# A two-layer graph network on one core: merges of gathered sums in two float32r parts, one more range of early products, and another planned landing time

## The chip, the cores and the metric

The kernel runs on one core of one Trainium2 chip. The metric is device time in microseconds for one execution. All timed runs compute the whole network, from the inputs in DRAM to the normalized output in DRAM.

## The reference

A graph isomorphism network (GIN) of two layers with a residual connection and a layer norm. There are N = 6250 nodes with D = 256 features, E = 100,000 edges sorted by destination, and a hidden width H = 512. Destinations are dense at low node numbers (node = 6250 u^2 for uniform u), sources are uniform.

```
def gin_agg(h, src, dst, eps):
    agg = segment_sum(h[src], dst, num_segments=N)
    return (1.0 + eps) * h + agg

h = gin_agg(x, src, dst, eps1)          # N x 256
h = relu(h @ W1a + b1a)                 # N x 512
h = relu(h @ W1b + b1b)                 # N x 512
h = gin_agg(h, src, dst, eps2)          # N x 512
h = relu(h @ W2a + b2a)                 # N x 512
y = x + (h @ W2b + b2b)                 # N x 256
out = (y - mean(y)) / sqrt(var(y) + 1e-5)
```

All values are float32.

## The kernel before, in words

**Tiles.** Nodes are cut into 49 tiles of 128 rows. The eight lowest tiles ("heavy") receive about 40% of the edges. For them no row is gathered: layer 1 counts, for every source node and every heavy destination node, how many edges go from one to the other (`counting`, one-hot matmuls), and the sums of heavy tiles are then products of this count matrix with the rows. The products of layer 1 (`first_products`, L1823) run in two passes of four heavy tiles each; each pass waits for its counts. The edges of all other tiles, 474 chunks of 128, are gathered by indirect DMA that GpSimd issues (L525), 128 rows at a time; in layer 1 five of the chunks are loaded row by row by the sync engine instead, so 469 are gathered there and 474 in layer 2.

**Sums of gathered rows.** Chunks form groups. For each group a one-hot matrix `sel` and a placement matrix `to` are made on VectorE. TensorE sums gathered rows into 32-row slots of a PSUM bank (L1206), and `merge` moves this partial sum to node rows: ScalarE copies it from PSUM to `split`, TensorE multiplies it with `to` (L1269), and VectorE adds the result to the accumulators of the tiles that the group reaches (L1279). In layer 1 a merge takes two groups at a time, 2 x 256 columns, with a float32 copy and one float32 matmul a group; the profile records each float32 matmul as two. In layer 2 a merge takes one group of 512 columns, and the copy rounds to float32r; VectorE subtracts it from the bank (L1260) and gives the second, lower part, and two float32r matmuls add up both parts.

**Dense work.** When all contributions of a block of one or two tiles are in, `dense` transposes it (L1323), multiplies with the first weight (L1392) and the second (L1425), and finishes: in layer 1 bias and relu on VectorE and ScalarE and a store of h1 to DRAM from ScalarE's queue (L1442); in layer 2 residual, layer norm and the store of the output from the sync queue.

**Products of layer 2** (`second_products`). The 49 source tiles are 13 ranges of four (the last has one tile). For each range its rows of h1 are loaded (`xr`, sync queue, L1510; two buffers), split into two float32r parts `upper` and `xr` by ScalarE and VectorE (L1587, L1588, L1592), the counts are loaded (`ci`, sync queue, L1613) and cast by ScalarE to `cf` (L1631), and for each of the eight heavy tiles one group of up to eight matmuls of 512 columns is run (L1704) and added to `whole_acc` (L1649; the first time a copy, L1644). The first `AHEAD2` ranges in the order 12, 11, 10, ... are done within layer 1, at priority 6, the lowest; the rest in layer 2 at priority 3. Within layer 1, from shortly before the last gathered rows are planned to have landed (`quiet`), no further product, cast or split of these is placed until the last dense block of layer 1 is placed (`settled`). The buffers `xr` and `upper` turn round over both layers: a range takes the buffer of the range two before it.

**Order.** Nothing of this order is chosen at run time. Each engine runs its instructions as they were written, and a planner (`Plan`) writes them: it plays all processes against a model of costs. A process asks for an engine with a cost and a priority (`("on", "PE", cost, priority)`, lower goes first), for a buffer (`"get"`), or for an event (`"until"`). Gathers are modelled by a pace (`GATHERS`) and a time from the end of the last issue of a piece to its landing (`LANDINGS`, for layer 1 and layer 2). A piece is up to four gathers; six pieces have a place, and the gather that reuses a place waits for the sum that read it. In layer 2 up to three pieces are summed in one turn. SP issues its loads in the order in which the planner came to them, and a load that waits holds back those behind it.

**Between the layers.** The first 24 gathers of layer 2 (`fore`) read h1 without tiles 7 and 8, which are the last ones that layer 1 stores; the contribution of these two tiles is added by matmuls (`adding_late`). So these gathers can start when all other tiles are stored. A zero row of h1 stands in for rows of tiles 7 and 8.

The planner's constants that the change touches:

```
AHEAD2 = 3                # ranges of layer 2's products done in layer 1
LANDINGS = (5.0, 6.0)     # planned landing after the issue, layer 1, layer 2
```

Of the kernel before, what the change touches and what calls it, by code (L numbers as in the profile page):

```python
# [17 lines left out]
P = 128  # L18
# [24 lines left out]
SPLITS = 2  # L43
TILES = 2
# [11 lines left out]
AHEAD2 = 3  # L56
# [15 lines left out]
def dve(n):  # L72
    return 0.085 + 0.00105 * n
# [126 lines left out]
LANDINGS = (5.0, 6.0)  # L200
# [14 lines left out]
BEGINS = (0.0, -40.0)  # L215
FREES = ({"PE": 20.0, "DVE": 22.0, "ACT": 24.0}, {"PE": -4.0, "DVE": -4.0, "ACT": -4.0})
# [159 lines left out]
def tile_gin_residual_layernorm(  # L376
# [176 lines left out]
    def opening(prep, bank, at):  # L553
# [31 lines left out]
        empty = prep.tile([1, H], F32, name="empty")  # L585
        nc.vector.memset(empty, 0.0)
        nc.scalar.dma_start(h1[GAP : GAP + 1, :], empty)
# [22 lines left out]
        def zeroing(of, i):  # L610
            k = slice(i * size, min((i + 1) * size, NT))
            to = of[:, k, :].bitcast(F32)
            nc.scalar.activation(
                to, zero_[:, 0:1].unsqueeze(2).to_broadcast(list(to.shape)), AF.Copy
            )

        for i in range(ZEROS):
            zeroing(at[0], i)
        for i in range(EARLY):
            zeroing(at[1], i)  # L620
# [78 lines left out]
        sloti = prep.tile([P, NCP - NC2], I, name="sloti")  # L699
        nc.vector.tensor_scalar(sloti, dsti, SLOTS - 1, None, op0=ALU.bitwise_and)  # L700
        nc.vector.tensor_copy(slot, sloti)
# [8 lines left out]
        within = prep.tile([P, NG], I, name="within")  # L710
        nc.vector.tensor_scalar(within, headi, SLOTS - 1, None, op0=ALU.bitwise_and)
        turn = prep.tile([P, NG], I, name="turn")
        nc.vector.scalar_tensor_tensor(turn, within, part32, above, op0=ALU.is_gt, op1=ALU.add)
        turned = prep.tile([P, NG], I, name="turned")
        nc.vector.tensor_scalar(turned, turn, PARTS - 1, None, op0=ALU.bitwise_and)
        nc.vector.tensor_scalar(home, turned, float(SLOTS), part32, op0=ALU.mult, op1=ALU.add)
# [5 lines left out]
        wb = prep.tile([P, NG], I, name="wb")  # L722
        nc.vector.tensor_scalar(wb, basei, P - 1, None, op0=ALU.bitwise_and)
        own = prep.tile([P, NG], F32, name="own")
        nc.vector.scalar_tensor_tensor(own, wb, part, tb, op0=ALU.is_gt, op1=ALU.add)
# [101 lines left out]
    def ordered(ctx):  # L827
# [45 lines left out]
        def layer(number, pools, table, width, scale, weights, ba, wide, at=None, aside=None, right=None):  # L873
# [50 lines left out]
            def fetch_rows(i):  # L924
# [13 lines left out]
            to_room = Tiles(keep, [P, 2, P], F32 if once else F32R, "to", 5)  # L938
            split_room = Tiles(
                keep if once else hold, [P, 2, width], F32 if once else F32R, "split",  # L940
# [300 lines left out]
            def merge(gs, shared):  # L1241
                ap = bank[shared.number]
                n = len(gs)
                token = yield ("get", split_room, 0)
                split = token.tile
                yield ("on", "ACT", act(n * width), 0)
                if once:
                    if gs[0][2] == gs[-1][2]:
                        used = gs[0][2]
                        nc.scalar.copy(  # L1250
                            split[:used, :n, :].rearrange("p a b -> p (a b)"), ap[:used, : n * width]
                        )
                    else:
                        for i, (g, to, used, _) in enumerate(gs):
                            nc.scalar.copy(split[:used, i, :], ap[:used, i * width : (i + 1) * width])
                else:
                    used = gs[0][2]
                    nc.scalar.copy(split[:used, 0, :], ap[:used])  # L1258
                    yield ("on", "DVE", dve(width), 0)
                    nc.vector.tensor_tensor(  # L1260
                        split[:used, 1, :], ap[:used], split[:used, 0, :], op=ALU.subtract
                    )
                shared.release()
                united = yield ("get", banks, 0)
                yield ("on", "PE", MERGE[number - 1] + n * width * (4 if once else 2) * PASS, 1)
                pu = bank[united.number]
                for i, (g, to, used, to_token) in enumerate(gs):
                    for l in (i,) if once else range(2):
                        nc.tensor.matmul(  # L1269
                            pu[:, i * width : (i + 1) * width], to[:used], split[:used, l, :],  # L1270
                            start=(once or l == 0), stop=(once or l == 1),
                        )
                    to_token.used()
                token.release()
                for i, (g, to, used, _) in enumerate(gs):
                    for t in reach(g):
                        yield ("until", ready[t])
                        yield ("on", "DVE", dve(width), 1)
                        nc.vector.scalar_tensor_tensor(  # L1279
                            acc[t], pu[:, i * width : (i + 1) * width], mask[:, t - lo[g], g : g + 1],  # L1280
                            acc[t], op0=ALU.mult, op1=ALU.add,
                        )
                        settle(t)
                united.release()
# [1265 lines left out]
```

## Time and profile before

| | us |
|---|---|
| median of 3 runs | 1271.05 |
| lowest, highest | 1269.08, 1276.44 |
| the profiled execution | 1268.54 |
| its span, first to last instruction | 1266.8 |

| engine | busy us | share of the span | instructions |
|---|---|---|---|
| TensorE matmul (PE) | 1179.4 | 93% | 6204 |
| TensorE weight load (PEld) | 777.3 | 61% | 6204 |
| VectorE (DVE) | 819.1 | 65% | 2096 |
| ScalarE (ACT) | 654.2 | 52% | 1367 |
| GpSimd (POOL) | 906.8 | 72% | 956 |

The profile is of one execution. Times in its rows are microseconds from the start of the span, durations of single instructions are nanoseconds where a row says "mean ns". Matmuls are pipelined: the time that one costs in a row of them is the distance from start to start, not its duration. Layer 1 fills the span up to about 626, layer 2 the rest. PEclk is the granted TensorE clock as a share of full speed. `q` behind an engine's name means its queue, which issues DMAs and waits.

### The profile page before, as it was taken

The page shows a single profiled execution, that of the slowest core. Times are in us where ns is not written, and L with a number is a line of the kernel's source. Part 1 is how long each engine was busy: PE and PEld are TensorE (multiplying, and loading weights), DVE is VectorE, ACT ScalarE, POOL GpSimd, SP SyncE. Part 2 cuts the span into 40 slices and gives each one's busy share as a digit, 9 for nine tenths or more (in the row PEclk, how much of TensorE's full clock was granted, in tenths as well). Part 3 has the DMA queues.
Part 4 walks back from the last instruction along what each step waited for, and adds up shares of the span by engine and source line. Part 5 has one row for each costly group of instructions (what it writes and reads, how often), then busy time and mean ns, then how long its engine had stood idle before and what let it go on. Part 6 is the DMA issues. An engine that isn't in the chain of part 4 may idle for free. (4 is left out here: it accounts for less than half of the span.)

```text
span 1266.8 us, 21197 instructions
## 1 busy us (share of the span) xinstructions
PE 1179.4 (93%) x6204; PEld 777.3 (61%) x6204; DVE 819.1 (65%) x2096; ACT 654.2 (52%) x1367; POOL 906.8 (72%) x956
## 2 busy tenths in 40 slices
PE   5879899999999999999789899999979999999997
PEld 4345455665555665566446675767756766777676
DVE  7989998878769643333257668769846556645424
ACT  7756679987885764444354334334324434432122
POOL 6777777777777777776477777777777777777730
PEclk9989999999999999999979999999999999999999
DMA  6445466775457776654598888889888888877741
GB/s 213 142 139 151 127 196 202 213 210 159 148 156 210 212 222 202 224 185 128 165 318 301 287 281 273 249 287 308 272 301 259 285 289 254 284 226 243 211 134 48
DMA packets 137646, 276.06 MB, mean 218 GB/s; under 512 B 21754, under 2 KB 68673, under 8 KB 137526
## 3 DMA queue, kind: packets, MB, share of 16 engines
q0 software_dynamic: 60432, 185.79, 48.0%
q1 hardware_dynamic: 43012, 56.43, 13.3%
q10 hardware_dynamic: 34082, 32.43, 7.9%
q8 instruction: 52, 0.85, 0.3%
q14 instruction: 68, 0.56, 0.1%
HBM read 248.95 MB, written 25.62 MB: 217 GB/s over the span
## 5 line engine op out<-in xcount | busy, mean ns | idle before, releaser
L525 POOL DMA_INDIRECT early<-in_x_dram,srcs x469 | 450.0, 960 | 146.4 <-issue 122.8
L525 POOL DMA_INDIRECT early<-h,places x226 | 216.8, 959 | 68.9 <-issue 57.9
L525 POOL DMA_INDIRECT late<-h,places x224 | 214.4, 957 | 68.2 <-issue 56.7
L1279 DVE SCALAR_TENSOR_TENSOR acc<-bank,mask,acc 128x256 f32<-128x256 f32 (+1 forms) x352 | 201.4, 604 | 58.1 <-PE bank L1269 56.1
L1425 PE MATMUL bank<-w1b_s,ht 128*128 128x512 f32 (+1 forms) x392 | 183.6, 597 | 2.9 <-ACT ht L1402 1.9
L1704 PE MATMUL bank<-upper,cf 128*128 128x512 f32 (+1 forms) x392 | 172.3, 440 | 0.9 <-DVE xr L1592 0.9
L1704 PE MATMUL bank<-xr,cf 128*128 128x512 f32 (+1 forms) x392 | 158.2, 404 | 0.6 <-DVE xr L1592 0.5
L1392 PE MATMUL bank<-zt,w2a_s 128*128 128x256 f32 (+2 forms) x736 | 151.2, 359 | 1.2 <-ACT zt L1351 1.2
L1206 PE MATMUL bank<-early,sel 128*32 128x256 f32 (+1 forms) x1414 | 125.8, 470 | 26.5 <-DMA early<-h,places 9.9
L1392 PEld LDWEIGHTS bank<-zt,w2a_s 128*128 128x128 f32 x736 | 127.7, 191 | 27.1 <-ACT split L1258 5.0
L1631 ACT CAST cf<-ci 128x512 fp32r<-128x512 uint8 (+1 forms) x104 | 61.4, 594 | 156.4 <-PE bank L1704 126.6
L1649 DVE TENSOR_TENSOR whole_acc<-bank,whole_acc 128x512 f32<-128x512 f32 x96 | 65.1, 683 | 77.2 <-PE bank L1704 77.1
L1823 PE MATMUL bank<-cf,xh 128*128 128x512 f32 x392 | 110.5, 420 | 4.6 <-DVE xh L1762 4.5
L1425 PEld LDWEIGHTS bank<-w1b_s,ht 128*128 128x128 f32 (+1 forms) x392 | 71.1, 189 | 67.6 <-issue 57.5
L1894 ACT ACTIVATE ca<-numbers,low 128x128 f16<-128x128 f16 x308 | 98.1, 391 | 26.7 <-PE bank L1946 22.5
L1269 PE MATMUL bank<-split,to 128*128 128x512 f32 (+2 forms) x332 | 99.3, 416 | 9.6 <-ACT split L1250 6.2
L1060 DVE TENSOR_TENSOR sel<-iota,slot 128x256 f32<-128x256 f32 (+2 forms) x112 | 49.1, 439 | 90.6 <-PE bank L1206 86.4
L1402 ACT ACTIVATE ht<-bank,b2a_s 128x256 f32<-128x256 f32 (+2 forms) x92 | 36.9, 446 | 134.4 <-PE bank L1392 134.4
L1206 PEld LDWEIGHTS bank<-early,sel 128*32 128x32 f32 x1414 | 38.4, 111 | 101.3 <-issue 57.9
L1392 PE MATMUL bank<-zt,w1a_s 128*128 128x256 f32 (+2 forms) x432 | 96.6, 369 | 3.8 <-ACT zt L1351 2.5
L1915 DVE TENSOR_SCALAR cb<-numbers,si 128x490 f16<-128x490 f16 (+8 forms) x308 | 89.0, 332 | 7.6 <-PE bank L1946 7.3
L1704 PEld LDWEIGHTS bank<-upper,cf 128*128 128x128 f32 (+1 forms) x392 | 75.8, 193 | 25.4 <-issue 4.3
(205 smaller groups left out, 1822.1 us busy)
## 6 DMA issues: line engine op xcount, KB each, us to landing
raw<-in_x_dram ACTq DMA_DIRECT2D x48, 256.0 KB
h<-h1r ACTq DMA_DIRECT2D x48, 256.0 KB
b2b_c<-in_x_dram SPq DMA_DIRECT2D x640, 1.0 KB
xr<-h SPq DMA_DIRECT2D x10, 1024.0 KB
acc<-h SPq DMA_DIRECT2D x17, 512.0 KB
early<-in_x_dram,srcs POOLq DMA_INDIRECT x469
ci<-counts SPq DMA_DIRECT2D x24, 256.0 KB
acc<-in_x_dram SPq DMA_DIRECT2D x21, 256.0 KB
```

The source lines that it names most:

```text
L525: nc.gpsimd.indirect_dma_start(out=rows_[:, j, :], out_offset=None, in_=table, in_offset=bass.IndirectOffsetOnAxis(ap=rows_in[:, c - first ...
L1206: mm = nc.tensor.matmul(pm[b * SLOTS : (b + 1) * SLOTS], sel[:, c - groups[g][0], :], rows_[:, l, :], start=(c == part[0]), stop=(c == par ...
L1269: nc.tensor.matmul(pu[:, i * width : (i + 1) * width], to[:used], split[:used, l, :], start=(once or l == 0), stop=(once or l == 1),)
L1279: nc.vector.scalar_tensor_tensor(acc[t], pu[:, i * width : (i + 1) * width], mask[:, t - lo[g], g : g + 1], acc[t], op0=ALU.mult, op1=ALU.add,
L1392: nc.tensor.matmul(ph[:, (f - o) * TILES * P : (f - o) * TILES * P + nb], wa[:, k, f * P : (f + 1) * P], zt[:, k, :nb], start=(k == 0), st ...
L1425: nc.tensor.matmul(po[:m], ht[:, f, i * P : i * P + m], wb[:, f, :], start=(f == 0), stop=(f == KH - 1),)
L1631: nc.scalar.copy(cf_token.tile[:, : n * P].rearrange("p (k j) -> p k j", j=P), token.tile[:, :n, a : a + P],)
L1649: nc.vector.tensor_tensor(sums_of[t], bank[token.number][:, :width], sums_of[t], op=ALU.add)
L1704: nc.tensor.matmul(bank[token.number][:, :width], cf[:m, j * P : (j + 1) * P], of[:m, j, :], start=(j == 0 and of is upper), stop=(j == le ...
L1823: nc.tensor.matmul(bank[tokens[f].number][:, :c], xh[:m, j, l, f * P : (f + 1) * P], cf[:m, :c], start=(k == 0 and l == 0), stop=(k == NT ...
L1894: nc.scalar.activation(token.tile[:, j, :], numbers[:, :P], AF.Abs, bias=low[:, q * BATCH + j : q * BATCH + j + 1],)
L1915: made = nc.vector.tensor_scalar(token.tile[:, : NT * width_of[c]], numbers[:, : NT * width_of[c]], spot[:, c : c + 1], None, op0=ALU.is_e ...
```

## The change

It does five things.

1. In layer 1, merges that the planner places after 160 us (`PARTED`) use the scheme of layer 2: ScalarE's copy rounds to float32r, VectorE subtracts it from the bank for a second part, and two float32r matmuls a group replace the one in float32. A merge of two groups makes one copy and one subtraction over 512 columns where both groups use the same number of rows. Earlier merges stay in float32. `split` gets room for both parts of both groups (`SIZE`), `to` is float32r in both layers, and layer 1 has four `to` buffers where it had five.
2. `AHEAD2` is 4: range 9 of layer 2's products is placed in layer 1 too, after ranges 12, 11 and 10.
3. `LANDINGS` for layer 2 is 9.0: the planner takes gathered rows to land 3 us later than before.
4. The zero row of h1 is stored from a cleared part of the counts tile instead of a tile of its own; the store moves on ScalarE's queue from ahead of the `dst` loads to behind the clearing of the counts.
5. Five integer tiles of the opening are overwritten in place.

```diff
-AHEAD2 = 3
+AHEAD2 = 4
-LANDINGS = (5.0, 6.0)
+LANDINGS = (5.0, 9.0)
+SIZE = (2, 1)
+PARTED = 160.0
...
-        empty = prep.tile([1, H], F32, name="empty")
-        nc.vector.memset(empty, 0.0)
-        nc.scalar.dma_start(h1[GAP : GAP + 1, :], empty)
...
         for i in range(ZEROS):
             zeroing(at[0], i)
+        empty = at[0][0:1, : size - size % 4, : H].bitcast(F32)
+        n = min(H // empty.shape[2], empty.shape[1])
+        assert n * empty.shape[2] == H
+        nc.scalar.dma_start(
+            h1[GAP : GAP + 1, :].rearrange("a (k n) -> a k n", n=empty.shape[2]), empty[:, :n, :]
+        )
...
-            to_room = Tiles(keep, [P, 2, P], F32 if once else F32R, "to", 5)
+            to_room = Tiles(keep, [P, 2, P], F32R, "to", 4 if once else 5)
             split_room = Tiles(
-                keep if once else hold, [P, 2, width], F32 if once else F32R, "split",
+                keep if once else hold, [P, 2, SIZE[number - 1] * width], F32R, "split",
                 SPLITS if once else 3,
             )
...
-                if once:
-                    if gs[0][2] == gs[-1][2]:
...
+                if gs[0][2] == gs[-1][2]:
+                    parts = [(gs[0][2], slice(0, n * width))]
+                else:
+                    parts = [
+                        (used, slice(i * width, (i + 1) * width))
+                        for i, (g, to, used, _) in enumerate(gs)
+                    ]
+                parted = not once or plan.now > PARTED
+                for used, at_ in parts:
+                    to_ = split[:used, 0, at_]
+                    nc.scalar.copy(to_ if parted else to_.bitcast(F32), ap[:used, at_])
+                if parted:
+                    yield ("on", "DVE", dve(n * width), 0)
+                    for used, at_ in parts:
+                        nc.vector.tensor_tensor(
+                            split[:used, 1, at_], ap[:used, at_], split[:used, 0, at_],
+                            op=ALU.subtract,
+                        )
                 shared.release()
                 united = yield ("get", banks, 0)
-                yield ("on", "PE", MERGE[number - 1] + n * width * (4 if once else 2) * PASS, 1)
+                yield (
+                    "on", "PE", MERGE[number - 1] + n * width * (2 if parted else 4) * PASS, 1
+                )
...
-                    for l in (i,) if once else range(2):
+                    at_ = slice(i * width, (i + 1) * width)
+                    for l in range(2) if parted else (0,):
+                        lhs, rhs = to[:used], split[:used, l, at_]
+                        if not parted:
+                            lhs, rhs = lhs.bitcast(F32), rhs.bitcast(F32)
                         nc.tensor.matmul(
-                            pu[:, i * width : (i + 1) * width], to[:used], split[:used, l, :],
-                            start=(once or l == 0), stop=(once or l == 1),
+                            pu[:, at_], lhs, rhs, start=(l == 0), stop=(l == 1 or not parted),
                         )
```

## Rows read from the trace of the kernel before

**Rows 1.** The page's chain that ended last, shares of the span by engine.

```profile
PE 35%; DVE 6%; DMA 4%; POOL 2%; issue 1%; ACT 1%; DVEq 0%; ACTq 0%; POOLq 0%
```

**Rows 2.** Timeline of POOL: start, us, instruction, idle before and what ended it.

```profile
616.91 0.94 POOL L525 DMA_INDIRECT early<-h,fore  x1 [17.71 <-PE bank L1392]
...
1214.88 0.95 POOL L525 DMA_INDIRECT late<-h,places  x1 [0.30 <-issue]
```

**Rows 3.** Windows: stretch, length, each engine's busy us, PEclk, DMA share, GB/s.

```profile
160.00:400.00 240.00, 230.56 (x1240) 140.89 (x1241) 194.06 (x550) 201.57 (x462) 181.97 (x191) 1.00 0.62 184
500.00:607.00 107.00, 104.20 (x519) 65.86 (x518) 35.96 (x65) 45.52 (x96) 75.13 (x80) 0.98 0.56 177
626.00:640.00 14.00, 4.92 (x25) 0.62 (x24) 3.12 (x8) 2.59 (x5) 10.65 (x12) 0.65 0.99 351
640.00:700.00 60.00, 58.87 (x300) 36.54 (x297) 43.88 (x96) 32.46 (x61) 45.68 (x48) 0.94 0.90 305
945.00:1110.00 165.00, 163.59 (x870) 116.87 (x869) 99.69 (x202) 66.85 (x126) 124.80 (x133) 1.00 0.85 273
1216.00:1267.00 51.00, 42.85 (x302) 38.46 (x294) 15.76 (x47) 13.00 (x39) 0.00 (x0) 0.98 0.12 39
```

**Rows 4.** Timeline of PE between the layers.

```profile
617.22 7.03 PE L1425 MATMUL bank<-w1b_s,ht 128*128 128x512 f32 x16
...
623.68 0.79 PE L1704 MATMUL bank<-upper,cf 128*128 128x512 f32 x1
...
625.71 0.40 PE L1704 MATMUL bank<-xr,cf 128*128 128x512 f32 x1
627.40 1.07 PE L1206 MATMUL bank<-early,sel 128*32 128x512 f32 x8 [1.29 <-issue]
633.87 1.94 PE L1206 MATMUL bank<-early,sel 128*32 128x512 f32 x8 [5.41 <-DMA early<-h,fore]
...
640.06 0.80 PE L1704 MATMUL bank<-upper,cf 128*128 128x512 f32 x1
```

**Rows 5.** Timeline of the sync queue there; idle between merged issues is inside.

```profile
609.51 17.00 SPq L1510 DMA_DIRECT2D xr<-h  x2
626.62 15.39 SPq L1613 DMA_DIRECT2D ci<-counts  x3
```

**Rows 6.** Timeline of ACT there.

```profile
637.41 0.62 ACT L1631 CAST cf<-ci 128x512 fp32r<-128x512 uint8 x1 [11.77 <-DMA ci<-counts]
```

**Rows 7.** Windows of line 1269 alone: PE and PEld busy (records).

```profile
160.00:400.00 240.00, 18.89 (x72) 13.04 (x72) 1.00 0.62 184
400.00:612.00 212.00, 9.93 (x38) 7.11 (x38) 0.99 0.62 189
```

**Rows 8.** Chain of waits in order of time: start, us, what.

```profile
674.94 7.48 PE bank L1704 x32
...
783.42 3.45 PE bank L1392 x16
...
1254.85 1.78 PE bank L1392 x16
```

**Rows 9.** Groups of layer 2 by line and shape: busy, mean ns, idle before.

```profile
L1260 DVE TENSOR_TENSOR split<-bank,split 128x512 fp32r<-128x512 f32 x82 | 53.4, 682 | 16.2 <-ACT split L1258 16.2
...
L1631 ACT CAST cf<-ci 128x512 fp32r<-128x512 uint8 x80 | 49.4, 619 | 124.8 <-PE bank L1704 107.2 <-DMA ci<-counts 11.8 <-issue 5.0
```

**Rows 10.** Line 1704 alone: ns min/median/max, first and last start us.

```profile
L1704 PE MATMUL bank<-upper,cf x392: 389/396/988, 532.6 to 1201.1; 128*128 128x512 f32 x192, 106*128 106x512 f32 x4
```

**Rows 11.** What PE waited for in layer 2: us, times, longest.

```profile
PE bank L1206 <- DMA early<-h,places: 9.9, 4, 4.8
...
PE bank L1206 <- DMA late<-h,places: 1.8, 1, 1.8
```

**Rows 12.** Timeline of PE near the end.

```profile
1223.21 0.71 PE L1269 MATMUL bank<-split,to 128*128 128x512 f32 x2
...
1241.21 0.60 PE L1323 MATMUL bank<-ident,apart 128*128 128x128 f32 x4
```

More of the change, by code (lines that the diff above doesn't have):

```diff
@@ L698, in opening @@
         nc.vector.tensor_copy(dsti, dp[:, : NCP - NC2])
-        sloti = prep.tile([P, NCP - NC2], I, name="sloti")
-        nc.vector.tensor_scalar(sloti, dsti, SLOTS - 1, None, op0=ALU.bitwise_and)
-        nc.vector.tensor_copy(slot, sloti)
+        nc.vector.tensor_scalar(dsti, dsti, SLOTS - 1, None, op0=ALU.bitwise_and)
+        nc.vector.tensor_copy(slot, dsti)
         nc.vector.tensor_tensor(
@@ L709, in opening @@
         nc.vector.tensor_scalar(above, headi, 5, None, op0=ALU.arith_shift_right)
-        within = prep.tile([P, NG], I, name="within")
-        nc.vector.tensor_scalar(within, headi, SLOTS - 1, None, op0=ALU.bitwise_and)
+        nc.vector.tensor_scalar(headi, headi, SLOTS - 1, None, op0=ALU.bitwise_and)
         turn = prep.tile([P, NG], I, name="turn")
[L713 to L716, printed above, removed]
+        nc.vector.scalar_tensor_tensor(turn, headi, part32, above, op0=ALU.is_gt, op1=ALU.add)
+        nc.vector.tensor_scalar(turn, turn, PARTS - 1, None, op0=ALU.bitwise_and)
+        nc.vector.tensor_scalar(home, turn, float(SLOTS), part32, op0=ALU.mult, op1=ALU.add)
         basei = prep.tile([P, NG], I, name="basei")
@@ L721, in opening @@
         nc.vector.tensor_scalar(tb, basei, 7, None, op0=ALU.arith_shift_right)
-        wb = prep.tile([P, NG], I, name="wb")
-        nc.vector.tensor_scalar(wb, basei, P - 1, None, op0=ALU.bitwise_and)
+        nc.vector.tensor_scalar(basei, basei, P - 1, None, op0=ALU.bitwise_and)
         own = prep.tile([P, NG], F32, name="own")
-        nc.vector.scalar_tensor_tensor(own, wb, part, tb, op0=ALU.is_gt, op1=ALU.add)
+        nc.vector.scalar_tensor_tensor(own, basei, part, tb, op0=ALU.is_gt, op1=ALU.add)
         nc.vector.tensor_tensor(own, own, lowest, op=ALU.subtract)
@@ L1246, in merge @@
                 yield ("on", "ACT", act(n * width), 0)
-                if once:
-                    if gs[0][2] == gs[-1][2]:
-                        used = gs[0][2]
-                        nc.scalar.copy(
-                            split[:used, :n, :].rearrange("p a b -> p (a b)"), ap[:used, : n * width]
-                        )
[L1253 to L1262, printed above, removed]
+                if gs[0][2] == gs[-1][2]:
[5 more added lines that the diff above has]
+                    ]
```

## The prediction

> **What bounds the kernel now.** I read the chain of waits first, then the queues of the two ends, then stages. The chain that ended last starts in layer 2 and goes through TensorE for 35% of the span, through gathers in GpSimd for 2% [rows 1]: from about 640 us on matmuls decide. GpSimd's own rows say what else is fixed: it issues gathers at an even pace, stops once for 17.71 us between the layers, and issues the last one at 1214.88 [rows 2], some 52 us before the span's end. The table by stage [rows 3] then shows where TensorE has room: in 500 to 607 it is busy 104.20 of 107 us, in 945 to 1110 163.59 of 165, but between the layers (626 to 640) 4.92 of 14. So two saturated stretches with a hole between, and what is taken from the second shortens the end only if it isn't paid for before its start.
>
> How the hole comes about matters most here. Layer 1's last dense matmul group starts at 617.22; one group of layer 2's products (eight L1704 matmuls, 623.68 to 625.7) runs behind it; then TensorE has only sums of early gathers until its first own product of layer 2 at 640.06 [rows 4]. The sync queue tells why: two loads of xr stand in one row that begins at 609.51 and lasts 17.00 us, and the loads of counts stand behind, at 626.62 [rows 5]. The second xr load wants the buffer of layer 1's last range, so it leaves when that range's last product is done, and the counts, which queue behind it, land so that ScalarE's first cast waits 11.77 us, until 637.41 [rows 6]. Hence the rule I use: **layer 2's products start about 14.4 us (640.06 less 625.7) after layer 1's last product, whenever that is.**
>
> **The change, part by part.**
>
> *Merges.* Merges planned after 160 us are 72 + 38 = 110 matmul records of 256 columns in float32 [rows 7], two a group, so 55 groups in 28 merges. One record takes 3.45/16 = 0.216 us in the chain; a float32r matmul of 512 columns takes 7.48/32 = 0.234 [rows 8]. Two float32r parts of 256 columns replace two records. No row shows float32r at 256: if time goes with columns, 0.117 each and 110 x (0.216 - 0.117) = 10.9 us saved; if it does not, 0.234 each and 2.0 us lost. I take the first, since float32 goes with columns (16 records of 128 columns take 1.78 us, 0.111 each, half of 0.216 [rows 8]), and keep the second in the range. Against it stands a VectorE subtraction a merge: layer 2's own, 512 wide, takes 0.682 us [rows 9], so 28 x 0.682 = 19.1 us, some 18 of them (12.3 us) in 160 to 400, where VectorE is busy 194.06 of 240 us [rows 3]. The merge's matmuls wait for it, and sums and dense work queue behind them on TensorE. I therefore count 5 us of the 10.9 as gained (bounds -2.0 and 10.9): in 400 to 612 VectorE is free and 38 records give 3.8 us; of the 7.1 before, I let the new wait eat all but 1.2.
>
> *The fourth range.* 8 groups of 8 matmuls, 64 x 0.234 = 15.0 us, leave layer 2 and enter layer 1. With them go 8 count casts (0.619 us) and 4 casts with 4 copies, priced alike, on ScalarE, 9.9 us, 4 subtractions and 8 additions on VectorE, priced at 0.682, 8.2 us [rows 9], and on the sync queue one xr load and two counts loads. ScalarE and VectorE are busy 45.52 and 35.96 of 107 us in 500 to 607 [rows 3], so these cost nothing there; if the cover were gone they would cost their 9.9. TensorE is another matter. Layer 1's products begin only at 532.6 [rows 10], run at the lowest priority, and stop being placed shortly before the last gather has landed; three ranges are 24 groups, of which one already fell behind the last dense group [rows 4]. That stretch is full, so 8 more groups find only the 5 us that merges free: 2.7 groups. The other 5.3 groups, 10.0 us, go behind the one at 623.68. By the rule above layer 2's products then start at 650.1, and have 15.0 us less to do: net 15.0 - 10.0 = 5.0 us. The sums of gathers no longer wait behind products in a hole of the same length that lies 10 us later: two more of them (1.07 us each, as at 627.40 [rows 4]) fit in it, 2.1 us. Its slow clock (granted 0.65 in 626 to 640, 0.94 after [rows 3]; the lower level is 1.2 GHz, after a stretch with little work) I leave unchanged.
>
> *Landings planned at 9 us.* The order puts each sum of layer 2 about 3 us later against its gathers. TensorE waited 9.9 + 1.8 us in layer 2 for gathers of places [rows 11]. A fixed order shifted by 3 us can fill 3 us of waiting in all, since gathers keep their pace; bounds 0 and 11.7; I take 3.0. The other sign is a buffer freed later, on which GpSimd's next gather waits. A piece's buffer comes round after six pieces, and in 945 to 1110 the gathers kept pace (133 of them, 124.80 us busy [rows 3]), so I price a stall at no more than the same 3 us once; and at the end it is covered: the last merge runs at 1223.21, but the transposes of a tile it fed start at 1241.21 [rows 12], since other dense work holds TensorE.
>
> *The rest.* One fewer `to` buffer in layer 1, in-place integers, and the zero row read from a cleared counts tile: 0. The store moves behind four clears on ScalarE and behind the dst loads on its queue; its first reader is the gather at 616.91 [rows 2], and a small VectorE or ScalarE operation more or less in the opening is worth at most one like those of [rows 9], 0.7 us to either side.
>
> **Sum.** 5.0 + 2.1 + 3.0 = 10.1 us, made against 1268.54 us of the profiled execution (its span of 1266.8 and 1.7 around it): 1258.4. The median of the runs is 1271.05, 2.5 above; minus 10.1 it is 1260.9. I write 1260.
>
> Against the sum stands a weight load share of 116.87 in 165 us, 71%, beside 99% for matmuls, in 945 to 1110 [rows 3]. The Trainium skill, Perfetto Trace Analysis, section Identifying the Most-Contended Engine, says that matmul busy share is not a good measure of how near TensorE is to its limit, and that the busy share of weight loads is better. By that rule there would be room in layer 2, the 15.0 us would be idle time, and the sum would be 0 (the first rival). By the row of 32 products at 0.234 us each, one behind the other [rows 8], there is none.
>
> **Rivals.**
>
> *Nothing comes of it.* If TensorE has room in layer 2, the 15.0 us become idle time and the end hangs on the last gather plus what follows it, which the change leaves: 1271. For it: weight loads fill 116.87 of 165 us [rows 3], and GpSimd keeps its pace. Against: the chain, and 1241.21.
>
> *Slower, by VectorE.* The new subtractions stand at the head of VectorE's order in the stretch where counting shares it. If their 12.3 us all delay counting, the second pass of layer 1's products, which wait for the counts, ends that much later, layer 2's early products start at 545 instead of 532.6, nothing of the 5 us is gained, and 27.3 us of groups instead of 10.0 stand behind the last dense group. Then 15.0 - 27.3 + 2.1 + 3.0 = -7.2: 1278. Once the 5 us are lost, it decides from a delay of 5.1 us (2.1 + 3.0). For it: 81% busy VectorE; against: TensorE, busy 230.56 of 240 there [rows 3], is fuller and gets relief.
>
> *More than that.* All 10.9 us of merges count, and all 11.7 of waiting: 10.9 + 2.1 + 11.7 = 24.7. But the gathers cap it: dense work that needs the last merge can start at most 18.0 us earlier (1241.21 less 1223.21 [rows 12]) unless the last gather itself comes earlier. So 1271 - 18 = 1253. For it: the hole may also shrink. Against: the fixed order, which turns little of the waiting into work.
>
> **How the numbers follow.** Forecast 0.47 (own range 1255 to 1266), nothing 0.20, slower 0.15, more 0.18. A measurement of this kernel can tell about 0.5%, 6.4 us, from no change: faster is below 1264.7, slower above 1277.4. Faster: 0.41 + 0.04 + 0.18 = 0.63; slower: 0.01 of nothing and 0.10 of the slower case, 0.11; the rest, 0.26, is same. The range 1249 to 1273 goes 4 us below the cap, for a last gather that comes earlier, and leaves out most of "slower" and the far part of "more", some 0.17.
>
> **What would show it.** Right: in layer 1 merges of four float32r records near 0.117 us apart; layer 1's last dense group still near 617, five to seven product groups behind it, xr's second load waiting for the last of them and counts behind it, first product of layer 2 near 650; 64 fewer L1704 matmuls in layer 2; fewer waits on gathers; span near 1257. Wrong: a first product at 640 (then the fourth range found room, and the gain is more), or counting that ends clearly after where it did and products after 540 (then VectorE took it back), or TensorE idle in 945 to 1110 with the same end (then it was never the bound), or gaps in GpSimd's pace.

## The result, and the profile after

The changed kernel takes 1261.75 us (median of 6 runs, 1259.48 to 1265.0) where the kernel before takes 1269.18 beside it: a ratio of 0.994 with an interval of 0.9914 to 0.9967, 7.4 us faster. Its profiled execution takes 1263.54 us, with a span of 1261.8. The forecast of 1260 came within 2 us; the way there was another than the sum's. Ratios leave out executions more than 1.5% above the fastest of the same kernel. (Lines have moved: a gather is L527 now, a sum of gathered rows L1207, a merge L1278, dense work L1400 and L1433, a product of layer 2 L1712, the load of xr L1518, of counts L1621.)

The page's chain, to hold against [rows 1]:

```profile
PE 35%; DMA 6%; POOL 3%; DVE 2%; issue 2%; ACT 0%; POOLq 0%; DVEq 0%
```

The shares hardly tell the two kernels apart; where the chain leaves the gathers does. First the end of the chain before (start, us, what):

```profile
1204.67 4.95 DMA early<-h,places
...
1223.93 8.81 PE bank L1392 x64
...
1247.76 5.36 PE bank L1392 x48
```

and the chain after:

```profile
1224.34 5.19 DMA late<-h,places
...
1229.66 1.07 PE bank L1207 x8
...
1241.07 5.36 PE bank L1400 x48
```

Before, the last gather (1214.88 [rows 2]) isn't in the chain. The chain leaves an earlier one, which lands at 1209.6 (TensorE waited 3.5 us for gathers just there), and 57 us of sums, dense work and layer norm follow: by the order as written, TensorE was behind. After, the last gather itself is the link, and 37 us of sum, merge and dense work follow it without a wait. GpSimd's timeline, beside [rows 2]:

```profile
621.27 0.94 POOL L527 DMA_INDIRECT early<-h,fore  x1 [21.24 <-PE bank L1400]
...
640.69 1.33 POOL L527 DMA_INDIRECT late<-h,fore  x1 [4.72 <-issue]
...
1224.34 1.12 POOL L527 DMA_INDIRECT late<-h,places  x1 [0.30 <-issue]
```

Layer 2's gathers begin 4.4 us later (616.91 before), stop once for 4.72 us, which is new, and end 9.5 us later. Before, the first gather into `late` came without a stop:

```profile
632.17 1.10 POOL L525 DMA_INDIRECT late<-h,fore  x1 [0.30 <-issue]
```

TensorE between the layers, beside [rows 4]:

```profile
621.77 7.03 PE L1433 MATMUL bank<-w1b_s,ht 128*128 128x512 f32 x16
628.24 0.80 PE L1712 MATMUL bank<-upper,cf 128*128 128x512 f32 x1
...
639.56 0.39 PE L1712 MATMUL bank<-xr,cf 128*128 128x512 f32 x1
641.29 1.92 PE L1207 MATMUL bank<-early,sel 128*32 128x512 f32 x16 [1.35 <-issue]
647.26 0.59 PE L1712 MATMUL bank<-upper,cf 128*128 128x512 f32 x1 [4.04 <-ACT upper L1595]
```

Layer 1's last dense group starts 4.6 us later, and six groups (48 matmuls) stand behind it in place of one. The sync queue waits for the last of them, as in [rows 5]:

```profile
614.14 26.21 SPq L1518 DMA_DIRECT2D xr<-h  x2
640.46 0.91 SPq L1621 DMA_DIRECT2D ci<-counts  x2
```

and ScalarE's first cast for the counts behind it, as in [rows 6]:

```profile
646.07 0.62 ACT L1639 CAST cf<-ci 128x512 fp32r<-128x512 uint8 x1 [12.89 <-DMA ci<-counts]
```

By stage (columns as in [rows 3]):

```profile
500.00:607.00 107.00, 101.09 (x504) 62.59 (x497) 41.76 (x76) 49.36 (x102) 75.77 (x80) 0.97 0.58 181
626.00:640.00 14.00, 13.95 (x55) 9.99 (x53) 4.84 (x7) 3.87 (x6) 7.57 (x8) 1.00 0.69 219
...
945.00:1110.00 165.00, 160.24 (x847) 114.73 (x840) 94.45 (x193) 61.09 (x115) 125.30 (x131) 0.98 0.84 273
```

The hole of 626 to 640 is full of products, and has moved behind them. In 500 to 607 TensorE is idle 5.9 us, 2.8 before: part of what merges freed there stayed free. In 945 to 1110 it now has 4.8 us to spare, where it had 1.4, while GpSimd issues its gathers at the same pace: work has left TensorE and the gathers have not come earlier.

### The profile page after: what moved, and what is told of

The parts are those of the page before. It is cut to its first block, busy times and chain, and to the rows that moved or that the text cites. A ratio compares the mean times of both kernels' runs of the same rounds, so it can differ in the third digit from the quotient of the medians.

```text
span 1261.8 us, 21174 instructions
## 1 busy us (share of the span) xinstructions
PE 1173.7 (93%) x6204; PEld 775.9 (61%) x6204; DVE 832.2 (66%) x2123; ACT 653.5 (52%) x1367; POOL 908.6 (72%) x956
## 5 line engine op out<-in xcount | busy, mean ns | idle before, releaser
L527 POOL DMA_INDIRECT early<-in_x_dram,srcs x469 | 450.9, 961 | 146.3 <-issue 126.2
L527 POOL DMA_INDIRECT early<-h,places x226 | 216.4, 958 | 68.9 <-issue 54.5
L527 POOL DMA_INDIRECT late<-h,places x224 | 216.1, 965 | 68.2 <-issue 57.6
L1433 PE MATMUL bank<-w1b_s,ht 128*128 128x512 f32 (+1 forms) x392 | 183.7, 595 | 0.4 <-ACT ht L1410 0.4
L1712 PE MATMUL bank<-upper,cf 128*128 128x512 f32 (+1 forms) x392 | 171.2, 437 | 8.7 <-ACT cf L1639 4.6
L1712 PE MATMUL bank<-xr,cf 128*128 128x512 f32 (+1 forms) x392 | 158.4, 404 | 2.7 <-DVE xr L1600 2.7
L1400 PE MATMUL bank<-zt,w2a_s 128*128 128x256 f32 (+2 forms) x736 | 152.0, 360 | 0.7 <-ACT zt L1359 0.7
L1400 PEld LDWEIGHTS bank<-zt,w2a_s 128*128 128x128 f32 x736 | 128.9, 192 | 25.5 <-issue 3.3
L1207 PE MATMUL bank<-early,sel 128*32 128x256 f32 (+1 forms) x1414 | 124.7, 467 | 18.9 <-DMA early<-h,places 6.2
L1433 PEld LDWEIGHTS bank<-w1b_s,ht 128*128 128x128 f32 (+1 forms) x392 | 71.6, 190 | 60.6 <-issue 52.9
L1278 PE MATMUL bank<-split,to 128*128 128x512 f32 (+2 forms) x332 | 92.4, 397 | 15.4 <-ACT split L1258 7.6
L1400 PE MATMUL bank<-zt,w1a_s 128*128 128x256 f32 (+2 forms) x432 | 97.2, 371 | 4.8 <-ACT zt L1359 3.8
L1258 ACT CAST split<-bank 128x512 fp32r<-128x512 f32 (+1 forms) x111 | 63.6, 583 | 66.3 <-PE bank L1207 53.1
L1712 PEld LDWEIGHTS bank<-upper,cf 128*128 128x128 f32 (+1 forms) x392 | 75.3, 192 | 33.1 <-ACT upper L1595 5.8
L1207 PEld LDWEIGHTS bank<-early,sel 128*32 128x32 f32 x1414 | 38.3, 110 | 91.1 <-issue 45.5
```

The source lines that it names most:

```text
L527: nc.gpsimd.indirect_dma_start(out=rows_[:, j, :], out_offset=None, in_=table, in_offset=bass.IndirectOffsetOnAxis(ap=rows_in[:, c - first ...
L1207: mm = nc.tensor.matmul(pm[b * SLOTS : (b + 1) * SLOTS], sel[:, c - groups[g][0], :], rows_[:, l, :], start=(c == part[0]), stop=(c == par ...
L1258: nc.scalar.copy(to_ if parted else to_.bitcast(F32), ap[:used, at_])
L1278: nc.tensor.matmul(pu[:, at_], lhs, rhs, start=(l == 0), stop=(l == 1 or not parted),)
L1400: nc.tensor.matmul(ph[:, (f - o) * TILES * P : (f - o) * TILES * P + nb], wa[:, k, f * P : (f + 1) * P], zt[:, k, :nb], start=(k == 0), st ...
L1433: nc.tensor.matmul(po[:m], ht[:, f, i * P : i * P + m], wb[:, f, :], start=(f == 0), stop=(f == KH - 1),)
```

## The experiments

Two theories. **P**: TensorE's work, in a row with the hole between the layers, sets the end, as the prediction had it. **G**: the end is layer 2's first gather, plus the row of its 474 gathers with any stall in it, plus a tail that can't fall below the 37 us of work behind the last gather. A ratio compares with the kernel before on the same chip. The result was measured where that takes 1269.18 us, and the experiments on three chips where it takes 1269.72, 1597.49 and 1633.19. Why the last two are slower is open (see the end), so from them only ratios, and what the order of the program explains, are used.

**The parts alone.** Merges only, on the 1270 us chip:

```diff
-AHEAD2 = 4
+AHEAD2 = 3
-LANDINGS = (5.0, 9.0)
+LANDINGS = (5.0, 6.0)
```

> Only the merges in two float32r parts, without the fourth range and with the landings planned as before; run again on another chip. By the prediction's sum the merges give 5.0 us less 2.1 us of the hole that they fill no more: about 1267, ratio 0.996 to 0.998. If the hidden half of the merges is all that there is (TensorE has no more work taken away than VectorE and ScalarE have added): 1.000. The first run of it gave 0.9986.

Measured: 1272.97 us, ratio 1.0027 (1.0010 to 1.0043): slower, if by little, and above both figures expected. GpSimd's timeline has the reason:

```profile
620.94 0.94 POOL L527 DMA_INDIRECT early<-h,fore  x1 [22.11 <-DMA xr<-h]
...
635.93 1.13 POOL L527 DMA_INDIRECT late<-h,fore  x1 [0.30 <-ACT upper L1595]
...
1218.95 0.95 POOL L527 DMA_INDIRECT late<-h,places  x1 [0.30 <-issue]
```

There is no stall, but the first gather is 4.0 us later. All 144 products lie before the last dense group here (136 before, with 8 behind it), which is 8 x 0.234 = 1.9 us of the 4.0. And the time that merges freed was not used. TensorE in 500 to 607:

```profile
500.00:607.00 107.00, 100.72 (x496) 62.72 (x495) 38.33 (x70) 42.52 (x88) 74.83 (x79) 0.97 0.54 164
```

It is idle 6.3 us, 2.8 before [rows 3]; the largest wait of it there is this one (us, times, longest):

```profile
PE bank L1712 <- ACT cf L1639: 3.8, 1, 3.8
```

The fourth range only:

```diff
-LANDINGS = (5.0, 9.0)
+LANDINGS = (5.0, 6.0)
-PARTED = 160.0
+PARTED = 1e9
```

> Only the fourth range of layer 2's products in layer 1, merges and landings as before; run again on another chip. By the prediction's sum 15.0 us move and 10.0 us of them fall behind layer 1's last dense group, so 5.0 us are gained: ratio 0.996. If the products behind the last dense group cost nothing, since they lie where TensorE would otherwise wait for layer 2's first counts: up to 15 us gained, ratio 0.988. If layer 2's gathers wait for the last product behind it (in the first run GpSimd stood still 11.4 us): 5 us or less, ratio 0.996 to 1.000. The first run of it gave 0.993.

Measured: 1272.38 us, ratio 1.0021 (1.0003 to 1.0039). Nothing is gained, and the ratio is above every case expected. Its profiled execution, 1268.6, is among its fastest. GpSimd's timeline:

```profile
614.71 0.95 POOL L527 DMA_INDIRECT early<-h,fore  x1 [15.62 <-PE bank L1400]
...
640.87 1.27 POOL L527 DMA_INDIRECT late<-h,fore  x1 [11.46 <-issue]
...
1222.07 0.95 POOL L527 DMA_INDIRECT late<-h,places  x1 [0.30 <-issue]
```

The first gather is 2.2 us earlier, but nine groups (72 products) stand behind the last dense group, and GpSimd stands still for 11.46 us before its first gather into `late`. With the merges too, six groups do, and the stall is 4.72; with one group or none there is no stall. In all seven traces that have the stall with `late` in this place, the gather starts 0.7 us after the last of these products has ended (in the changed kernel 639.56 + 0.39, and 640.69).

**The hole taken away.** The second xr load is issued behind the first counts:

```diff
                     for r in rs:
                         ks = ranges[r]
+                        if not once and r == rs[1]:
+                            yield ("rest", max(0.0, 3.0 - plan.now))
                         xr_token = yield ("get", xr_room, 0)
```

> The changed kernel, but layer 2's second load of its own rows (xr), which rests in the sync queue for layer 1's last product, is issued behind the first load of counts (ci), the sown rows and the apart sums' loads. So ci no longer stands behind a waiting load. Theory P (TensorE's work in a row, with its holes, sets the end): the hole between layer 1's last product and layer 2's first, 7.5 us in the changed kernel, mostly closes and the time falls by 5 to 7 us against the changed kernel (ratio to the kernel before about 0.989). Theory G (the start of layer 2's gathers and their row up to the last one, with a fixed tail behind it, set the end): the hole closes, TensorE waits for gathers as much longer later on, and the time stays within 2 us of the changed kernel's (ratio about 0.994).

Measured: 1262.62 us, ratio 0.9946 (0.9926 to 0.9966), as the changed kernel. The hole closed in part (lines are two further on: L1714 is the product):

```profile
641.96 0.40 PE L1714 MATMUL bank<-xr,cf 128*128 128x512 f32 x1
...
645.57 0.50 PE L1714 MATMUL bank<-upper,cf 128*128 128x512 f32 x1
```

From the last product of layer 1 to the first of layer 2 it is 3.6 us, 7.7 in the changed kernel, and products start 1.7 us earlier although layer 1's last product came 2.4 us and the first gather 3.3 us later, which stays unexplained. The times alone don't tell P from G: P's 5 to 7 us were for a start that much earlier, and 1.7 us is less than the executions of one kernel differ by. The waits and the chain do. TensorE waits longer in layer 2 for gathered rows. In the changed kernel:

```profile
PE bank L1207 <- DMA late<-h,places: 7.0, 3, 3.0
PE bank L1207 <- DMA early<-h,places: 6.2, 4, 4.1
```

and here:

```profile
PE bank L1207 <- DMA late<-h,places: 11.9, 8, 3.9
PE bank L1207 <- DMA early<-h,places: 10.4, 8, 2.3
PE bank L1207 <- DMA late<-h,fore: 4.0, 3, 1.8
```

26.3 us in place of 13.2, and the chain still leaves the last gather:

```profile
1225.29 4.58 DMA late<-h,places
```

This is what G expected and P did not.

**The stall taken away.** Layer 2's pools are opened in another order, so that `late` lies in other memory:

```diff
-            leave, hold, keep = (
+            leave, keep, hold = (
-                for name in ("leave2", "hold2", "keep2")
+                for name in ("leave2", "keep2", "hold2")
```

> The changed kernel, but layer 2's buffer `late` lies where other layer 1 memory lay (two pools of layer 2 are opened in the other order), so the first gather into it need not wait for layer 1's last product. Theory G: the 4.7 us in which GpSimd stood still before that gather go, the last gather starts some 4.4 us earlier and the time falls by about 4 us against the changed kernel (ratio to the kernel before about 0.991). Theory P: the stall goes, but TensorE's first 50 us of layer 2 don't use the rows so early; less than 1.5 us, ratio about 0.994. If the stall only moves to the other pool's first user, nothing changes and this run tells nothing.

Measured: 1257.18 us, ratio 0.9907 (0.9881 to 0.9933). GpSimd's timeline:

```profile
620.98 0.94 POOL L527 DMA_INDIRECT early<-h,fore  x1 [21.09 <-PE bank L1400]
...
635.96 0.95 POOL L527 DMA_INDIRECT late<-h,fore  x1 [0.30 <-issue]
...
1218.91 0.97 POOL L527 DMA_INDIRECT late<-h,places  x1 [0.30 <-issue]
```

and its chain's end:

```profile
1218.91 4.63 DMA late<-h,places
...
1235.10 5.36 PE bank L1400 x48
```

The last gather starts 5.4 us earlier, the same 37 us follow, and the median falls by 4.6 us. So the stall came from where `late` lies: the first gather into it had to wait until layer 1 was done with that memory. TensorE's first product of layer 2 comes 1.8 us later than in the changed kernel (647.26), and still the end is earlier, so that start doesn't set it and P falls:

```profile
649.07 0.80 PE L1712 MATMUL bank<-upper,cf 128*128 128x512 f32 x1 [5.95 <-ACT upper L1595]
```

This kernel is the fastest of those run on the 1270 us chips. The two were not run side by side and their intervals overlap; the timeline shows which 5 us are gone.

**The account.** The span is the first gather, plus the time to the last one, plus the tail. That holds by definition; what tells is which part moved, in the six traces of the 1270 us chips, in us from the timelines of GpSimd:

```
                     first gather   to the last   tail     span
before                     616.91        597.97   51.9   1266.8
merges only                620.94        598.01   53.2   1272.1
fourth range only          614.71        607.36   44.7   1266.8
changed kernel             621.27        603.07   37.5   1261.8
hole taken away            624.58        600.71   37.8   1263.1
stall taken away           620.98        597.93   37.1   1256.0
```

598 us is the row of gathers without a stall (with the hole taken away it still holds one of 3.8 us; with the fourth range only, the row makes up 1.8 us of its stall). 37 is the tail with nothing late on TensorE. Before, 15 us of the tail were TensorE's backlog. The change works that off and pays 4.4 and 5.1 us of it back on GpSimd.

Which part of the change works it off is not separated here: the three tails of 37 us all have the landings planned at 9 us, the other three at 6 us, and merges with range at 6 us was not run on such a chip. On the two slower chips, in one trace each, the tail is 59.5 us with merges only, 53.8 with landings only, 51.3 with range only, 48.6 and 48.1 with merges and range, and 46.1 to 46.4 with the range and landings at 9 us. There the fourth range takes off most of it, and the planned landings some 2 us on top.

**The same parts on the slower chips.** On the chip of 1597.49 us, the merges alone (the edit above):

> The change with its merges alone: three ranges in layer 1, landings planned at 6 us as before. Theory A (each part is worth what its term of the sum says, TensorE's work counts): merges free about 5 us of TensorE, the one product group behind layer 1's last dense group goes ahead of it, layer 2's products start 2 to 5 us earlier: 1264 to 1267 where before is 1269. Theory B (the parts only work together: without a fourth range the freed time is filled by nothing, since gathers end when they did): no change, 1268 to 1270.

Measured: ratio 0.9986 (0.9953 to 1.0019), no change, as in B. The range alone:

> The fourth range alone: merges of layer 1 stay in float32, landings at 6 us. Nine product groups stand behind layer 1's last dense group in program order, where the change has six and before has one. Theory A: 15 us of products move from layer 2 to a place 15 us ahead of it, so nothing is gained but the hole: 1266 to 1270. Theory B (the hole between the layers does not move as a whole but is filled): 9 groups take 16.8 us in what was a hole of 14 us, layer 2 starts only some 5 us later and has 15 us less to do: 1258 to 1262.

Measured: 0.9930 (0.9897 to 0.9964), as in B. The landings alone:

```diff
-PARTED = 160.0
+PARTED = 1e9
-AHEAD2 = 4
+AHEAD2 = 3
```

> Landings of layer 2 planned at 9 us, nothing else. Theory A: 3 us less, 1266, and less waiting of TensorE for gathers than the 11.7 us of before. Theory B (a fixed order shifted by 3 us only changes which wait comes first): 1268 to 1271, the waits for gathers within 3 us of before.

Measured: 0.9963 (0.9922 to 1.0004), which leaves A and B open. Merges and range, without the landings:

```diff
-LANDINGS = (5.0, 9.0)
+LANDINGS = (5.0, 6.0)
```

> The change without its third part: landings at 6 us again. Theory A: 3 us slower than the change, 1265. Theory B: as the change, 1261 to 1263. If the 4.7 us that GpSimd lost at 635 us hang on the planned landings, they are gone here; if they hang on the place of the second gather buffer, they stay.

Measured: 0.9888 (0.9831 to 0.9945), below both and nearer to B; the stall stays. GpSimd misses its pace all along there, so the account doesn't hold and the sizes don't carry over: the range alone gains there and not on the 1270 us chip. What does carry over is the stall before the first gather into `late`. Merges only:

```profile
818.40 1.23 POOL L527 DMA_INDIRECT late<-h,fore  x1 [0.30 <-issue]
```

the range only:

```profile
833.98 1.27 POOL L527 DMA_INDIRECT late<-h,fore  x1 [11.37 <-issue]
```

and both:

```profile
824.13 0.95 POOL L527 DMA_INDIRECT late<-h,fore  x1 [4.73 <-issue]
```

It is as long as on the 1270 us chip and doesn't need the landings.

**On the chip of 1633.19 us.** Merges and range again, by the last diff:

> The changed kernel with the landings of layer 2 planned as before (6 us in place of 9); merges and fourth range as in the change; run again on a chip where the kernel before takes 1270 us. The prediction's sum gave the planned landings 3.0 us: ratio to the kernel before 0.9965. Theory G (first gather of layer 2, its row of 943 - 469 gathers, the stall in it, and 37 us behind the last) has the changed kernel at its bound of 621.3 + 603.1 + 37.5 us, and this one has the same first gather and the same stall, so if TensorE's row is not later than that, nothing changes: 0.994. If TensorE then waits for landings as it did with the range alone (19.4 us in place of 13.2), its row ends later than the gathers' bound: about 1267, 0.998.

Measured: 0.9826 (0.9794 to 0.9858). Range and landings, without the merges:

```diff
-PARTED = 160.0
+PARTED = 1e9
```

> The changed kernel without the merges in two parts: fourth range and planned landings alone. Prediction's sum: 5.0 us of the gain go, ratio 0.996 + 0.002 = 0.998. Theory G: the first gather of layer 2 starts at 614.7 as with the range alone, GpSimd then stands still 11.5 us, last gather at 1222, bound 1259; TensorE's row is what counts, 1267 with the range alone, less what the planned landings save: 1262 to 1267, ratio 0.995 to 1.000. If the merges are worth nothing at the end of layer 1 (they made the first gather 4 us later when alone), this kernel is no slower than the changed one: 0.994 or less.

Measured: 0.9872 (0.9826 to 0.9917). The moved `late` (its diff above) and an earlier end of the filling:

```diff
-LEAD = 1.5
+LEAD = 14.0
```

> The changed kernel with two edits: the buffer `late` in other memory (as in the run that took GpSimd's stall away, 0.9907), and layer 1's filling by layer 2's products ended earlier, so that 136 products lie before the last dense group and 72 behind it, in place of 160 and 48. Theory G: 24 products of 0.234 us less before the last stores, so layer 2's first gather starts 5.6 us earlier, at 615.4, the last one at 1213.3, and the end comes at 1250 to 1252 unless TensorE's row, whose hole ends at 649 as before, sets it first: then 1254 to 1256. Ratio 0.986 to 0.990. Theory P: the same work in the same row with the same hole, no change against 0.9907.

Measured: 0.9811 (0.9770 to 0.9851). The first gather came 5.6 us earlier than with merges and range on the same chip, which has its landings at 6 us:

```profile
828.76 0.94 POOL L527 DMA_INDIRECT early<-h,fore  x1 [27.36 <-PE bank L1400]
```

and here, where the stall is back, though it was expected gone:

```profile
823.12 0.95 POOL L527 DMA_INDIRECT early<-h,fore  x1 [21.77 <-PE bank L1331]
...
847.49 0.95 POOL L527 DMA_INDIRECT late<-h,fore  x1 [9.65 <-DMA h<-h1r]
```

That is the 24 products of 0.234 us, but it can be chance: without the merges, also with 24 fewer products in front, the first gather came later on this chip, and 6.6 us earlier on the 1270 us chip.

```profile
833.06 0.94 POOL L527 DMA_INDIRECT early<-h,fore  x1 [24.59 <-PE bank L1400]
```

What holds the new place of `late` is open: the wait is put down to a store of h1, and the gather starts while products of layer 1 still run, until 852.3. And with the hole's edit (its diff above) added:

> The kernel of the line before with one edit more: layer 2's second load of its own rows issued behind the first load of counts, so that the hole in front of layer 2's products closes by some 7 us. If the gathers set the end in the kernel without this edit, nothing changes (within 2 us of it). If TensorE's row set it there, 3 to 7 us are gained: 1249 to 1251, ratio 0.984 to 0.986.

Measured: 0.9794 (0.9752 to 0.9836). All four ratios lie below the figures worked out for them from a 1270 us chip, so they test neither theory's sizes. The intervals of the last two and of merges with range overlap, so whether either edit is worth anything on top is not settled. Nor is the worth of the planned landings on a 1270 us chip.

## Why the prediction was right, and where not

**What bounds the kernel.** Right for the kernel before, where 15 us of the tail were work that TensorE was late with. Not seen: how far that carries. Gathers and the 37 us behind the last one would have ended at 616.91 + 597.97 + 37 = 1252, so a TensorE that becomes free gains 15 us and then nothing. The first rival, that the end hangs on the last gather and what follows it, describes the changed kernel well. Its time of 1271 was wrong because it took all 52 us of the tail for fixed.

**Merges.** The rate was right: a float32r matmul of 256 columns starts 0.119 us (median of 81 steps from record to record) after the one before, 0.117 expected, 0.216 in float32. But 29 of the 81 steps are 0.19 us or longer, so less than the 10.9 us comes free. TensorE's busy time with merges, beside [rows 7]:

```profile
160.00:400.00 240.00, 15.03 (x72) 10.33 (x72) 0.99 0.62 185
400.00:612.00 212.00, 7.81 (x36) 5.50 (x36) 0.98 0.64 196
```

is 6.0 us less. The step that failed is the 5 us counted as gained, above all the 3.8 us in 400 to 612 where VectorE is free: there TensorE waits 4.6 us for a cast instead (3.8 in the kernel with merges only). The products run earlier (from 517.3 on, 532.6 before [rows 10]) and so run into counts that are not loaded yet: the cast itself waits, for a load that stands behind forty row loads on the sync queue.

```profile
554.60 0.79 PE L1712 MATMUL bank<-upper,cf 128*128 128x512 f32 x1 [4.55 <-ACT cf L1639]
553.92 2.17 ACT L1639 CAST cf<-ci 128x512 fp32r<-128x512 uint8 x4 [10.85 <-DMA ci<-counts]
523.88 26.47 SPq L2217 DMA_DIRECT2D b2b_c<-in_x_dram  x40
550.45 0.36 SPq L1621 DMA_DIRECT2D ci<-counts  x1
```

Before, these counts leave that queue at 552.63, and TensorE has no such wait. Alone the merges lose 3.3 us. The bound of -2.0, which came from the matmul's rate, missed that. The rival by VectorE falls: counting ends 1.6 us later (380.9, 379.3 before), but the second pass starts at 383.2 as before (383.0), and the products come earlier, not later.

**The fourth range.** 6 groups behind the last dense group, 6.3 expected. The rule held in its cause, the xr load that waits for the last product with the counts queued behind it, and was wrong in its size: 7.7 us from last to first product, not 14.4, because the counts were cast 5.6 us after their issue and not 10.8 (626.62 to 637.41 [rows 5, 6]). So products start at 647.3, not 650.1, and the sum would have been 2.8 us larger. But that start doesn't set the end: with the stall taken away it came 1.8 us later and the end 5 us earlier. What set it was not in the sum at all: the groups behind the last dense group hold `late`, and layer 1's end came later. The last dense group, expected near 617 still, starts at 621.77, and the first gather 4.4 us later than before. The 24 products more in front of it are 5.6 us of TensorE; that they are the whole cause isn't shown, since merges alone, with 8 more, lose 4.0 us there. "Gaps in GpSimd's pace" stood among the signs of a wrong prediction; the one stall that it priced, 3 us for a buffer freed later, was another. The 2.1 us for two more sums in the hole failed too: 24 sum matmuls ran in it before and 16 run now.

**Landings.** 3.0 us fewer waits for gathers are not in the trace: 13.2 us against 11.7 [rows 11]. In a kernel that the gathers bound, waits are slack and no measure of this term. The 7.8 us that TensorE waited before for the first gathers, in the hole, are in neither figure. On the end it stays open on these chips.

**Sum.** 10.1 us forecast, 5.0 measured between the two profiled executions, 7.4 between the medians. The backlog gave 14.5 us (51.9 to 37.5), near the 15.0 us of products that left layer 2, though the share of the planned landings in it is open, and GpSimd took 9.5 back. Both are larger than any of the sum's three terms; that the total came out near is luck.

**On the shares.** The weight loads' share that the prediction set against its sum was 116.87 of 165 us with TensorE the bound and is 114.73 with the gathers the bound. The Trainium skill, Perfetto Trace Analysis, section Identifying the Most-Contended Engine, judges TensorE's headroom by that share, beside the share of peak FLOPs, which no row here gives. Here neither the weight loads' share nor the matmul share (163.59 and 160.24) tells the two cases apart, and the chain's last link does.

## What to carry to other kernels

Look for every row that must run at a fixed pace (here the gathers) and add up when it starts, how long it takes and what follows its last piece; the difference to the span is all that relieving another engine can gain. When work is moved across a stage border, list the memory that it holds there and who reuses it, since the wait appears on the engine of the reuser, not on the one that was relieved. And a change whose sum is right can have parts that lose alone, as merges and range do here on the 1270 us chip: run them alone.

## What the runs showed of the hardware

The time from a load's issue to its use differs between the kernels: the first counts of layer 2 were cast 10.8 us after issue before (626.62 to 637.41, DMA engines 1.00 busy, 349 GB/s), 7.5 us after (640.37 to 647.88, 0.99, 341 GB/s) in the kernel whose stall was taken away, and 5.6 us after (640.46 to 646.07, 0.83, 287 GB/s) in the changed kernel, where GpSimd had stood still until 640.69. It went with the load on the DMA engines; these are three single loads, and no run varied the load by itself.

The chips differ by more than any edit here. On the chip of 1597 us, GpSimd's gathers take the same 0.95 us each, but now and then the engines stop together. A piece of the timeline of the kernel with merges and range there:

```profile
202.34 0.47 ACT L1410 ACTIVATE ht<-bank,b1a_s 128x256 f32<-128x256 f32 x1 [5.15 <-remote]
...
203.08 0.32 DVE L1923 TENSOR_SCALAR cb<-numbers,si 128x392 f16<-128x392 f16 x1 [4.93 <-remote]
...
203.84 0.81 PE L1954 MATMUL bank<-cb,ca 128*128 128x392 f16 x2 [5.23 <-ACT ht L1410]
```

Three engines stand still for about 5 us. What let ScalarE and VectorE go on is not on record (`remote`), and TensorE waits for ScalarE. Stops of more than 1.5 us of these three at once, from 60 us on, add up to 33 us in that trace and 11 in the changed kernel's, so they are a small part of the 301 us between the two spans. The cause of the rest, and of the stops, stays open.
